# A two-layer graph network with layer norms on one core: closing the rows of four batches by VectorE block turns, transfers over DRAM and GpSimd sums

## The chip, the cores and the metric

The kernel runs on one core of a Trainium2 chip. The metric is the device time of one execution in microseconds (us). A core has TensorE (PE, the matrix engine), VectorE (DVE), ScalarE (ACT), GpSimd (POOL) and SyncE (SP), whose queue issues nearly all DMAs here. Each engine works through its own queue of instructions in order and waits at an instruction until what it needs is there. SBUF is the working memory of 128 partitions, PSUM the accumulators that TensorE writes, in banks of 128 x 512 numbers.

## The reference, cut to what matters

There are 16 batches of 1024 nodes with 128 features, and one 1024 x 1024 adjacency matrix. All is float32.

```python
# layer 0
x = layernorm(x + einsum('nm,bmo->bno', adj, x @ weight) + bias)
# layer 1: five steps of a gated unit; both of its matrices are adj
def step(h):
    m = einsum('nm,bmd->bnd', adj, h)
    av = concatenate([m, m], axis=-1)
    u3 = h @ u3_w.T + u3_b
    z = sigmoid(av @ w3_w.T + w3_b + u3)
    r = sigmoid(av @ w4_w.T + w4_b + u3)
    hv = tanh(av @ w5_w.T + w5_b + (r * h @ u5_w.T + u5_b))
    return (1 - z) * h + z * hv
h = x
for _ in range(5): h = step(h)
out = layernorm(x + h)
```

The last line is what the change concerns: the state `h` after five steps is added to `x`, the result of layer 0, and each node's 128 features are normalized.

## The kernel before, in words

**Tiling.** Four batches make a quad, and there are four quads. Layer 0 runs over the quads first and leaves its result in DRAM (`saved`). Then, for each quad q, layer 1 runs its steps s = 0 to 4. A step is an aggregation over all four batches (`aggregate`, L375) and then, batch by batch (k = 0 to 3), the gates and the update of the state (`gates` L472, `update` L483).

**Aggregation.** The product with the adjacency matrix uses a fast scheme with seven products in place of eight, on two levels: `aggregate` runs four calls of `chain` (L323), named 12, 3, 67 and 54 after the outer products that they make. A chain has seven inner products in the order 1, 5, 6, 2, 7, 3, 4 (chain 54: 1, 5, 6, 2, 7, 4, 3), each some matmuls at L361. After each product comes its evacuation `after[a]` out of PSUM: copies by ScalarE for products 1, 5, 6, 2 and 4, additions by VectorE for 7 (L351) and 3 (L352). `pb` is one bank that products 6, 7 and 4 share. The operands are sums that VectorE makes (`sums_of`, `outer_sums`, L286 to L321). The last sums, at L411 and L413, write the aggregate `agg`. Its right half of columns (`agg[:, k, HALF:]`) is written only at the end of an aggregation.

**Hooks.** What else is to be issued during an aggregation is passed in as `hooks`: for a chain, and for one of its seven products, a list of calls that are traced just before it ("end": after the last). This sets the program order. A scheduler then orders each engine's queue at compile time: of what it takes to be ready, the earliest in program order goes first, so that later work can move ahead into a gap. `tc.keep_in_program_order` ties an instruction behind the one traced before it on its engine, `pin` does so where `strict[0]` is set, and `tc.issue_after(i)` puts instructions on i's engine behind i.

**Two layouts.** The state lives as `hid`, features on partitions. The aggregation needs `rows`, nodes on partitions. Between steps `turn_rows` (L516) turns 32 x 32 blocks of `hid` with one VectorE instruction (L519) into a buffer (`ypad`), writes it to `turned` in DRAM (L523), and `fetch_rows` (L528) reads it back with four DMAs (L532) in such an order that the 128 x 128 turn is complete. `turn_hidden` (L536, turns at L542) and `fetch_hidden` (L551) go the other way for the state that a new quad starts from.

**Gates and update.** For half h of batch k: a matmul with `u3` into a PSUM bank (L451), copied by ScalarE to `seeded`; a matmul with `w4` on top (L462), a sigmoid (L465), a VectorE product (L466); one with `w3` (L467) and a sigmoid. The update has two matmuls (L479, L480), a tanh (L490) and three VectorE instructions (L496 to L498). The banks that `bank` (L92) hands out are three, for gates, updates and turns together.

**Closing rows.** After the last step of a quad, `finish_early` (L656) loads the batch's rows of layer 0 from `saved` into a buffer `y`. `finish` (L576) turns the state with TensorE, four 128 x 128 transposes by `ident` a half (L566), into a bank, and VectorE adds that to `y` (L574). `normalize` (L580) calls `layernorm` (L233): on VectorE eight pairs of `bn_stats` (L240) and `bn_aggr` (L242), on GpSimd four small instructions that make `rstd` and `shift` (L245 to L248), and the application in eight pieces. It goes onto the list `waiting` for ScalarE (L251), of which `drain` (L279) issues three, or one, after each product; with "DVE" it goes to VectorE at once (L261). The store (L257) follows. Batch 0 is closed in s=4 of its own quad, between update 1 and gates 3 (L748). Batches 1 to 3 are closed in s=0 of the next quad through hooks (L718 to L725). The last quad has an ending of its own (`ending`, L660), which keeps its turns and has the only large GpSimd instructions (L679, L680).

## Time and profile before

| what | value |
|---|---|
| three runs | 1811.39, 1811.89, 1814.22 us; median 1811.89 |
| the profiled execution | 1811.78 us, of which the span from first to last instruction is 1810.0 |
| TensorE's granted clock | 0.998 of full speed |
| TensorE turns for closing (L566) | 120 matmuls of 128 x 128, a duration of 281 ns each |
| VectorE additions of them (L574) | 30 of 128 x 512, 675 to 681 ns on average |
| VectorE turns to rows (L519) | 48 of 128 x 1024, 1248 ns; 32 of 128 x 512, 713 ns |
| VectorE turns to hidden of a new quad (L542, into `first`) | 48 of 128 x 256, 415 ns |
| GpSimd `rstd` (L246) | 31 of 128 x 8, 1758 ns |
| write to `turned`, median to landing | 512 KB, 3.8 us |
| fetch from `turned`, median to landing | 128 KB, 2.8 us |
| load of `ypad` from `saved`, median to landing | 512 KB, 3.8 us |

A line of the profile names the source line, the engine, the operation, the tile written and those read (out<-in), the shape, and the count. In a timeline the first number is the start in us from the span's start, the second the time until the group's last instruction ends. In brackets stands how long the engine was idle before it, and what ended that. Matmuls overlap with one another, so the time that one holds TensorE is the distance to the next one's start, not its duration.

### The profile page before, as it was taken

Reading aid. Unit: us, or ns where it says so; the run is one execution under the profiler, and the core shown is the slowest. Engines: PE = TensorE matmul, PEld = TensorE weight load, DVE = VectorE, ACT = ScalarE, POOL = GpSimd, SP = SyncE. Lnnn points to the kernel's source line nnn. Section 1 sums busy time; section 2 is a strip of 40 time slices with the busy share of each in tenths; the row PEclk is TensorE's granted clock in tenths of the full one; section 3 lists DMA queues with packets and bytes.
Section 4 is the critical chain, followed back from the end, with each engine's and each line's share of the span. In section 5 each row is a group of like instructions: output and inputs, shape, how many; then the busy total and the mean of one; then the engine's idle time right before and its main releaser. Section 6 shows DMA issues by size and latency. Waiting matters only on the chain.

```text
span 1810.0 us, 19922 instructions
## 1 busy us (share of the span) xinstructions
PE 1787.7 (99%) x6805; PEld 1269.2 (70%) x6805; DVE 1293.8 (71%) x2316; ACT 793.4 (44%) x1418; POOL 98.0 (5%) x142
## 2 busy tenths in 40 slices
PE   8999999999999999999999999999999999999998
PEld 7888884866758576675857757586675858667584
DVE  7987776676766958576676957667577775767667
ACT  2345555344342554434244463434434553443426
POOL 0112220000000010000000200000000100000004
PEclk9999999999999999999999999999999999999999
DMA  6233262140323334132142423214043331403222
GB/s 224 71 128 138 95 158 68 32 93 12 82 47 93 91 97 93 23 71 51 43 106 81 93 70 70 62 32 93 12 105 95 92 83 23 93 18 76 52 54 82
DMA packets 352564, 140.37 MB, mean 78 GB/s; under 512 B 338128, under 2 KB 339024, under 8 KB 352464
## 3 DMA queue, kind: packets, MB, share of 16 engines
q1 hardware_dynamic: 351600, 135.96, 29.5%
q10 hardware_dynamic: 864, 3.15, 0.4%
q8 instruction: 54, 0.88, 0.2%
q14 instruction: 46, 0.38, 0.1%
HBM read 80.35 MB, written 58.72 MB: 77 GB/s over the span
## 4 chain that ended last, share of the span: by engine, by line
PE 87%; DVE 7%; DMA 2%; ACT 1%; POOL 1%; issue 1%; SPq 0%; DVEq 0%; POOLq 0%
PE pb L361 23%; PE pa L361 13%; PE pc L361 12%; PE pu L462 7%; PE pu L451 7%; PE seeded L467 7%; PE ph L480 7%; PE ph L479 7%; PE pc_x L361 2%; PE pa_x L361 2%; PE seeded L428 1%; DMA rows<-saved 1%; POOL rstd L246 1%; PE pt L566 1%; DVE agg L411 1%
## 5 line engine op out<-in xcount | busy, mean ns | idle before, releaser
L361 PE MATMUL pb<-e,inner 128*128 128x256 f32 x864 | 206.7, 380 | 3.7 <-ACT pb L347 2.6
L466 DVE TENSOR_TENSOR tsum<-tsum,hid 128x512 f32<-128x512 f32 x160 | 107.1, 683 | 114.6 <-ACT tsum L465 114.2
L361 PEld LDWEIGHTS pb<-e,inner 128*128 128x128 f32 x864 | 167.1, 194 | 24.6 <-ACT pb L347 4.2
L490 ACT ACTIVATE tsum<-ph,bh 128x512 f32<-128x512 f32 x158 | 108.6, 687 | 145.0 <-PE ph L480 144.8
L462 PE MATMUL pu<-agg,w_t 128*128 128x512 f32 x320 | 166.0, 608 | 0.5 <-DVE agg L411 0.5
L480 PE MATMUL ph<-tsum,u_t 128*128 128x512 f32 x320 | 163.5, 592 | 0.1
L496 DVE TENSOR_TENSOR tsum<-tsum,hid 128x512 f32<-128x512 f32 x158 | 108.1, 684 | 77.6 <-ACT tsum L490 77.4
L479 PE MATMUL ph<-agg,w_t 128*128 128x512 f32 x320 | 163.5, 592 | 0.0
L467 PE MATMUL seeded<-agg,w_t 128*128 128x512 f32 x320 | 161.0, 592 | 0.0
L451 PE MATMUL pu<-hid,u_t 128*128 128x512 f32 x320 | 152.0, 594 | 2.0 <-DVE ypad L574 2.0
L361 PE MATMUL pb<-s,inner 128*128 128x256 f32 x576 | 151.3, 385 | 0.3 <-DVE agg L351 0.2
L361 PE MATMUL pb<-a,inner 128*128 128x256 f32 x576 | 144.6, 379 | 0.0
L465 ACT ACTIVATE tsum<-pu,br 128x512 f32<-128x512 f32 x160 | 110.2, 688 | 74.3 <-PE pu L462 69.9
L361 PE MATMUL pc<-e,inner 128*128 128x256 f32 x560 | 134.3, 379 | 0.3 <-DVE inner L288 0.3
L361 PEld LDWEIGHTS pb<-s,inner 128*128 128x128 f32 x576 | 108.7, 194 | 24.8 <-DVE rows L351 10.7
L470 ACT ACTIVATE tsum<-seeded,bz 128x512 f32<-128x512 f32 x160 | 109.9, 687 | 27.2 <-PE seeded L467 23.6
L361 PEld LDWEIGHTS pb<-a,inner 128*128 128x128 f32 x576 | 111.5, 194 | 14.1 <-issue 1.9
L361 PEld LDWEIGHTS pc<-e,inner 128*128 128x128 f32 x560 | 108.8, 195 | 12.3 <-PE pa L361 0.6
L498 DVE TENSOR_TENSOR hid<-hid,tsum 128x512 f32<-128x512 f32 x158 | 109.0, 690 | 10.1 <-DVE tsum L497 0.5
L480 PEld LDWEIGHTS ph<-tsum,u_t 128*128 128x128 f32 x320 | 60.7, 190 | 77.0 <-issue 72.9
L467 PEld LDWEIGHTS seeded<-agg,w_t 128*128 128x128 f32 x320 | 60.8, 190 | 76.6 <-issue 76.6
L479 PEld LDWEIGHTS ph<-agg,w_t 128*128 128x128 f32 x320 | 60.5, 190 | 75.4 <-issue 72.7
(181 smaller groups left out, 2859.3 us busy)
## 6 DMA issues: line engine op xcount, KB each, us to landing
turned<-ypad SPq DMA_DIRECT2D x48, 512.0 KB, 3.8
rows<-turned SPq DMA_DIRECT2D x192, 128.0 KB, 2.8
rows<-saved SPq DMA_DIRECT2D x20, 512.0 KB, 3.4
hid<-hidden SPq DMA_DIRECT2D x64, 128.0 KB, 3.4
turned<-ypad SPq DMA_DIRECT2D x32, 256.0 KB, 2.9
rows<-turned SPq DMA_DIRECT2D x128, 64.0 KB, 2.1
hid<-in_x_dram SPq DMA_DIRECT2D x12, 512.0 KB, 4.2
hidden<-first SPq DMA_DIRECT2D x24, 256.0 KB, 3.0
```

What stands on the lines that cost most here:

```text
L361: product = nc.tensor.matmul(bank_of[a][:, ts(o, QT)], chunk(a, o, c), left[n][a][:, c, :], start=(a in (1, 5) and o == 0 and c == 0), sto ...
L451: pin(nc.tensor.matmul(pu, w_t["u3"], hid[:, k, ts(h, HALF)], start=True, stop=True, skip_group_check=True))
L462: pin(nc.tensor.matmul(pu, w_t["w4"], agg[:, k, cols], start=False, stop=True, skip_group_check=True))
L465: pin(nc.scalar.activation(rh[:, cols], pu, AF.Sigmoid, bias=br))
L466: pin(nc.vector.tensor_mul(rh[:, cols], rh[:, cols], hid[:, k, cols]))
L467: pin(nc.tensor.matmul(pz, w_t["w3"], agg[:, k, cols], start=False, stop=True, skip_group_check=True))
L470: pin(nc.scalar.activation(z[:, cols], pz, AF.Sigmoid, bias=bz))
L479: pin(nc.tensor.matmul(ph, w_t["w5"], agg[:, k, cols], start=True, stop=False))
L480: pin(nc.tensor.matmul(ph, w_t["u5"], rh_of[k % 2][:, cols], start=False, stop=True))
L490: pin(nc.scalar.activation(hv, ph, AF.Tanh, bias=bh))
L496: pinned(nc.vector.tensor_sub(hv, hv, hid[:, k, cols]))
L498: pinned(nc.vector.tensor_add(hid[:, k, cols], hid[:, k, cols], hv))
```

## The change

For the first three quads, the closing turns leave TensorE. The state is turned by `turn_rows` as between steps, fetched back from `turned` into a buffer of its own (`close_fetch`, into `ypad`), and GpSimd adds it, in two halves, to the rows loaded from `saved` (`close_load`, `close_add`). `close` then calls `layernorm`. The buffers of the sums are now `hvs`, two pieces of `agg`'s right half, and `ypad[0]`. The places change too: in s=4 batches 0 and 1 are turned, fetched, loaded and summed, and batch 2 is turned. In s=0 of the next quad, hooks of chain 12 turn batch 3, fetch, load and sum batches 2 and 3, and issue the four `fetch_hidden` at products 2, 3 and 4 and the end; batches 1 and 2 are normalized at products 1 and 6 of chain 67, with their statistics pinned; batches 3 (applied on VectorE) and 0 after update 0. That update's `turn_rows` uses `first[:, 0]` in place of `ypad[0]`. VectorE's evacuations in chains are put behind the last statistic closed so far. `turn_hidden` makes one turn of 128 x 1024 and one DMA a batch where it made four turns and two DMAs. The last quad's ending stays as it was.

```diff
@@ def layernorm(y, tag, store, now=False):
-        n = y.shape[1]
+        if len(y.shape) == 4:
+            n = y.shape[1] * y.shape[2]
+            chunk = lambda c: y[:, c // y.shape[2], c % y.shape[2]]
+        else:
+            n = y.shape[1]
+            chunk = lambda c: y[:, c, :]
...
-                pin(nc.vector.bn_aggr(mv[:, c - 1, :], stats[:, c - 1, :]))
+                last_stats[0] = pin(nc.vector.bn_aggr(mv[:, c - 1, :], stats[:, c - 1, :]))
@@ def chain(...):
-            with tc.high_priority():
+
+            behind = tc.issue_after(closed[0].ins) if closed[0] else nullcontext()
+            with tc.high_priority(), behind:
                 after[a]()
@@ def update(tag, k, back=True, spare=False):
         if back and k < 3:
-            turn_rows(k)
+            turn_rows(k, stage=first[:, 0] if spare else None)
@@ def turn_rows(k, h=None, stage=None):
         cols, n = half_of(h)
-        t = ypad[k % 2][:, cols]
+        t = (ypad[k % 2] if stage is None else stage)[:, cols]
@@ def fetch_rows(k, h=None, dst=None):
         cols, n = half_of(h)
+        dst = rows[:, k] if dst is None else dst
         src = between(k, h).rearrange("(to n) (s j) x -> to j (n s) x", n=n, s=4)
         for to in range(4):
             tc.keep_in_program_order(nc.sync.dma_start(
-                rows[ts(to, SQ), k, cols].rearrange("j (m x) -> j m x", x=64), src[to]
+                dst[ts(to, SQ), cols].rearrange("j (m x) -> j m x", x=64), src[to]
             ))
@@ def turn_hidden(k, stage):
-        v = rows[:, k].rearrange("p (n c a j) -> p n c a j", n=4, c=2, a=4)
-        for f in range(2):
-            t = stage(f)
-            for a in range(2):
+        v = rows[:, k].rearrange("p (n c a j) -> p a n c j", n=4, c=2, a=4)
+        if len(stage) == 1:
+            t = stage[0].rearrange("p (a n i c) -> p a n c i", a=4, n=4, c=2)
+            nc.vector.transpose(t, v)
+        for f, t in enumerate(stage):
+            w = 4 // len(stage)
+            for a in range(w) if w < 4 else ():
                 nc.vector.transpose(
                     t[:, ts(a, QT)].rearrange("p (n i c) -> p n c i", n=4, c=2),
-                    v[:, :, :, 2 * f + a],
+                    v[:, w * f + a],
                 )
...
-    y_of = [ypad[0], ypad[1], hvs.rearrange("p h x -> p (h x)"), ypad[0]]
-
-    def finish_early(q, k):
-        nc.sync.dma_start(y_of[k], saved_rows(q * QUAD + k))
-        finish(q, k, y_of[k])
+    def pair(t):
+        return t.rearrange("p (u x) -> p u x", u=2)
+
+    y_of = [hvs, agg[:, 0:2, HALF:], agg[:, 2:4, HALF:], pair(ypad[0])]
+
+    def in_halves(b, src):
+        return src[b].rearrange("(p u c) d -> p u (c d)", u=2, c=CH)
+
+    def close_load(q, k):
+        src = saved[q * QUAD + k].rearrange("p (u x) -> p u x", u=2)
+        tc.keep_in_program_order(nc.sync.dma_start(y_of[k], src))
+
+    def close_fetch(k):
+        fetch_rows(k, dst=ypad[k % 2])
+
+    def close_add(k):
+        t = ypad[k % 2].rearrange("p (u n d c) -> p u n c d", u=2, n=2, c=2)
+        y = y_of[k].rearrange("p u (n c d) -> p u n c d", n=2, c=2)
+        for u in range(2):
+            tc.keep_in_program_order(nc.gpsimd.tensor_add(y[:, u], y[:, u], t[:, u]))
+
+    def close(q, k, now=False):
+        b = q * QUAD + k
+        store = in_halves(b, out).rearrange("p u (c d) -> p u c d", c=CH)
+        strict[0] = k in (1, 2)
+        layernorm(y_of[k].rearrange("p u (c d) -> p u c d", c=CH), f"1_{b}", store, now)
+        strict[0], closed[0] = False, last_stats[0]
@@ the loop over steps, s == 0 and q > 0
                     outer_sums(rows)
-                    before = [call(finish_early, q - 1, k) for k in range(QUAD)]
-                    norm = [call(normalize, q - 1, k, y_of[k]) for k in range(QUAD)]
-                    fetch = [call(fetch_hidden, k) for k in range(QUAD)]
+                    p = q - 1
                     hooks = {
-                        12: {5: [before[1]], 2: [fetch[0], before[2]], "end": [fetch[1], before[3]]},
-                        3: {1: [fetch[2]], 2: [fetch[3]]},
-                        67: {6: [norm[1]], 7: [norm[2]], 4: [norm[3]]},
-                        54: {"end": [call(drain, 99, 0)]},
+                        12: {
+                            1: [call(turn_rows, 3), call(close_fetch, 2)],
+                            5: [call(close_load, p, 2), call(close_add, 2)],
+                            6: [call(close_fetch, 3)],
+                            2: [call(fetch_hidden, 0)],
+                            7: [call(close_load, p, 3), call(close_add, 3)],
+                            3: [call(fetch_hidden, 1)],
+                            4: [call(fetch_hidden, 2)],
+                            "end": [call(fetch_hidden, 3)],
+                        },
+                        3: {},
+                        67: {1: [call(close, p, 1)], 6: [call(close, p, 2)]},
+                        54: {},
                     }
...
+            if last:
+                close_load(q, 0)
             gates(tag, 1)
-            update(tag, 0, not last)
-            if not last:
+            update(tag, 0, not last, s == 0 and q > 0)
+            if s == 0 and q > 0:
+                close(q - 1, 3, "DVE")
+                close(q - 1, 0)
+            if last:
+                turn_rows(0)
+                close_fetch(0)
+                close_add(0)
+            else:
                 fetch_rows(0)
             gates(tag, 2)
             update(tag, 1, not last)
             if last:
-                finish_early(q, 0)
-                normalize(q, 0, y_of[0])
+                turn_rows(1)
                 for k in range(2):
-                    turn_hidden(k, lambda f: first[:, k, ts(f, HALF)])
+                    turn_hidden(k, [first[:, k]])
             else:
                 fetch_rows(1)
             gates(tag, 3)
             if last:
                 sums_of(rows, (1, 2))
                 sums_of(rows, (3,))
                 for k in range(2):
-                    turn_hidden(2 + k, lambda f: first[:, k, ts(f, HALF)])
+                    turn_hidden(2 + k, [first[:, k]])
+                close_fetch(1)
+                close_load(q, 1)
+                close_add(1)
             update(tag, 2, not last)
+            if last:
+                turn_rows(2)
             update(tag, 3, not last)
```

## The prediction, made before the result was known

> **What bounds the kernel now.** I read the busy shares and the chain first, then stages by the table of windows, then the timeline where the changed work lies.
>
> ```profile
> PE 1787.7 (99%) x6805; PEld 1269.2 (70%) x6805; DVE 1293.8 (71%) x2316; ACT 793.4 (44%) x1418; POOL 98.0 (5%) x142
> PE 87%; DVE 7%; DMA 2%; ACT 1%; POOL 1%; issue 1%; SPq 0%; DVEq 0%; POOLq 0%
> ```
>
> TensorE (PE) is the bound, and its work is 87% of the chain. So a PE instruction that goes away counts in full, if nothing that replaces it makes PE wait. What closing rows costs is read from stages: a plain step, then the last step of the first quad (s=4), then the first step of the next (s=0).
>
> ```profile
> 467.17:544.34 77.17, 77.17 (x277) 53.32 (x276) 52.84 (x75) 31.45 (x52) 0.00 (x0) 1.00 0.25 55
> 544.34:620.77 76.43, 75.84 (x279) 53.20 (x278) 58.58 (x112) 29.41 (x49) 3.23 (x4) 1.00 0.40 101
> 620.77:703.62 82.85, 82.85 (x307) 55.81 (x306) 58.47 (x122) 45.66 (x87) 7.38 (x12) 1.00 0.34 85
> ```
>
> Columns: length, then busy time of PE, weight loads, VectorE (DVE), ACT, POOL, the clock, the DMA share, GB/s. The two closing steps take 76.43+82.85 = 159.28 us; two plain ones take 154.34. The excess is 4.94 us. At the other two changes of quads it is 76.15+82.85-154.34 = 4.66 and 77.57+82.86-154.34 = 6.09. Sum **15.7 us**: all that closing costs today on the bound. The timeline shows what it is made of:
>
> ```profile
> 606.93 1.11 PE L566 MATMUL pt<-ident,hid 128*128 128x128 f32 x8
> 607.88 1.12 PE L451 MATMUL pu<-hid,u_t 128*128 128x512 f32 x2
> 609.51 1.12 PE L451 MATMUL pu<-hid,u_t 128*128 128x512 f32 x2 [0.51 <-DVE ypad L574]
> ...
> 622.50 1.11 PE L566 MATMUL pt<-ident,hid 128*128 128x128 f32 x8
> 623.45 1.24 PE L361 MATMUL pc<-e,inner 128*128 128x256 f32 x5
> ```
>
> Eight turns hold PE from 606.93 to 607.88, and from 622.50 to 623.45: 0.95 us a batch, four a quad, 12 in all: 11.4 us. The rest, 4.3 us, is waiting: two L451 take 1.63 us (607.88 to 609.51) where two of that shape take 0.86 elsewhere, as PE waits for a PSUM bank that the turn holds until VectorE has added it (L574).
>
> **What the Trainium skill says.** "TensorE: Matmul & The Clock Gate", Part 4: a TensorE turn does a full 128x128, into PSUM, and needs a VectorE copy after it; the trace agrees (L566, then L574). "VectorE: DVE Perf Modes", The three transpose paths: VectorE turns 32x32 blocks only; hence the trip over DRAM. The trace has such turns (L519, 1248 ns for 128x1024). "SBUF — State Buffer", Who interferes with whom: a VectorE instruction with two SBUF inputs and a GpSimd (POOL) one that reads SBUF shut each other out. The trace agrees where both meet, in the ending:
>
> ```profile
> 1792.33 1.59 POOL L679 TENSOR_TENSOR first<-tsum,hid 128x512 f32<-128x512 f32 x1 [0.77 <-ACT tsum L470]
> 1793.14 1.33 DVE L466 TENSOR_TENSOR tsum<-tsum,hid 128x512 f32<-128x512 f32 x1 [0.35 <-ACT tsum L465]
> 1795.57 1.26 POOL L679 TENSOR_TENSOR first<-tsum,hid 128x512 f32<-128x512 f32 x1
> ```
>
> L466 takes 0.69 alone and 1.33 beside POOL; the POOL product takes 1.26 beside instructions with one input and 1.59 beside L466.
>
> **The change part by part.**
>
> *Turns of 12 batches removed from PE:* 12 x 0.95 = -11.4 us, and with the bank waits -15.7 us. All of it is on the path. Nothing new is put on PE, so the floor is 1811.8 (the profiled execution, 1810.0 of it span; the median is 1811.89) - 15.7 = 1796.1.
>
> *VectorE, per quad.* Removed: 8 additions from PSUM (two take 1.28: 5.1 us), 16 turns of 128x256 in `turn_hidden` (four take 1.43: 5.7). Added: 4 `turn_rows` (1.25 each: 5.0), 4 turns of 128x1024 for hidden (5.0, priced by the same row, the axis order being different), 8 `tensor_scalar` for batch 3 (four took 1.11 at L261: 2.2). Together 12.2 - 10.8 = +1.4 us, of no weight where it is spread. It moves, however: statistics of batch 0 (8 pairs, 2.3 us) leave s=4, which is the tightest place (VectorE 94% busy in its gates, 29.97 of 31.77 us in the table of windows), and those of 3 and 0 may fall in the gates of s=0. There VectorE is busy 25.17 of 34.92 us. There is cover before that too: with the sums and statistics of batches 1 to 3 done at 646.77, VectorE idles for long:
>
> ```profile
> 650.83 0.69 DVE L351 TENSOR_TENSOR rows<-pb,rows 128x512 f32<-128x512 f32 x1 [3.76 <-PE pb L361]
> ...
> 662.92 0.69 DVE L351 TENSOR_TENSOR rows<-pb,rows 128x512 f32<-128x512 f32 x1 [4.47 <-PE pb L361]
> ...
> 666.43 0.69 DVE L466 TENSOR_TENSOR tsum<-tsum,hid 128x512 f32<-128x512 f32 x1 [2.82 <-ACT tsum L465]
> ```
>
> Only batches 1 and 2 are pinned in program order, so those of 3 and 0 can float into these gaps. I take 0.3 us a quad, 0.9 in all; from 0 to 9.9 (rival B). `tensor_scalar` also waits for POOL's `rstd` (0.24+1.67 us); in a gap that costs nothing.
>
> *POOL sums:* 24 of 128x512, 1.26 to 1.6 us each, 30 to 38 us on an engine 5% busy. What counts is the lock: each can delay one VectorE addition by up to 1.33-0.69 = 0.64 us, 15.4 us in all if every delay reached PE, nothing if none does (a gain is excluded, since nothing else leaves POOL). A delay reaches PE only where VectorE is what PE waits for: in the plain weight-load waits that is mainly L351 (23 times) and L411 (17 times in 20 steps), so about one in ten: 1.8 us.
>
> *ACT:* batch 3 is applied on VectorE, 24 applications of 0.42 us less; ACT, 44% busy, is not the bound: 0.
>
> *DMA.* Per quad 4 writes and 16 fetches between SBUF and `turned` are added; the loads from `saved` and the stores stay. A plain step makes 4 such trips at a share of 0.25: 19.3 us of all engines. The two closing steps use 0.40x76.43+0.34x82.85 = 58.7 of 159 us; after it about 78 (49%). No queue fills up; what counts is lateness. On SyncE's (SP's) queue 20 issues of 0.38 to 0.48 us, some 9 us, stand among those of `fetch_hidden`, whose result is first used at 662.65, 42 us after the step's start: hidden.
>
> *The new waits.* Let T be the start of s=0 (620.77). `hid` of batch 3 is final at T+6.3 (627.0), its turn at T+7.5. SP waits for that turn first, since its write is issued ahead of the fetch of batch 2: fetch issued T+7.9 to T+9.9, landed T+12.7 (2.8), load from `saved` landed T+14.2 (3.8), two POOL sums T+17.4. SP then waits for POOL before loading batch 3 into the buffer batch 2 was fetched to: T+21.2, sums T+24.4. VectorE's queue is in order: statistics of 1 and 2 stand ahead of evacuation 7 of chain 67. That chain now starts at T+18.3 (21.1 less three turns), product 7 ends 5 x 1.72 later, at T+26.9; with 2.3 us of statistics, batch 2's sum may come as late as T+24.6. It comes at T+17.4: 7 us of slack. Behind the waiting instruction stand VectorE's evacuations, and PE behind those. Cost 0. The store of batch 2 leaves in chain 54, about T+36, and the buffer in `agg` is written at T+44: hidden.
>
> *Sum:* 1811.8 - 15.7 + 0.9 + 1.8 = 1798.8; **1799**.
>
> **Rivals.**
> A (0.60): as computed, 1796 to 1803.
> B (0.17): VectorE becomes the bound at the end of s=0. Statistics of 3 and 0 (4.6) and the `tensor_scalar` (2.2) all run after update 0, where the idle gaps left are 1.58+1.86 = 3.4 us: 3.4 us a quad reach the next step's sums. In place of the 0.3 taken above: 1798.8 + 3 x 3.1 = 1808. For it: program order puts them there. Against: they are ready earlier, and today's statistics already run some 10 us ahead of their place.
> C (0.08): every POOL lock reaches PE: 1796.1 + 15.4 = 1811.5, no difference. Against: VectorE has 29% idle time.
> D (0.15), slower: batch 2's (or a floated batch 3's) sum comes late, and VectorE's queue stands still with evacuation 7 behind it. It decides from T+24.6 on, each us counting three times; slower by over 0.2% needs 6.4 us more, T+31. If the 16 hidden fetches (16 x 0.48 = 7.7 us of issue, and 9.6 of transfer, half of a trip's 4.8 for each batch) stand ahead in SP's queue, the sum comes at T+34.7, 10.1 us late: 1798.8 + 30.3 = 1829. For it: SP's queue is in order, and the scheduler's estimate of landings decides what stands ahead. Against: six of the 16 are issued by T+4 today, and none of the new fetches waits for them by its data.
>
> **How the numbers follow.** 0.2% (3.6 us) is about what a measurement of this kernel can tell from no change. Faster: A and B, 0.77; same: C, 0.08; slower: D, 0.15. The range runs from the floor, 1796, over A, B and C to 1813; D and a little of the tails stay out. A alone is 1796 to 1803.
>
> **What would show it.** Right: L566 counts 24; the two closing steps take 155 to 156 us together; PE waits of L451 on `ypad` gone; POOL sums of 1.3 to 1.6 us. B: the first sums of s=1 late, PE waiting for `inner`. D: a VectorE idle stretch ahead of `bn_stats`, released by POOL. Wrong altogether: a wait for `hid` at the gates of s=0.

## The result, and the profile after

| what | before | after |
|---|---|---|
| median, range | 1813.06 us, 1811.39 to 1814.33 (4 runs) | 1859.75 us, 1857.85 to 1863.28 (4 runs) |
| the profiled execution, its span | 1811.78, 1810.0 | 1863.28, 1861.5 |
| TensorE turns for closing | 120 (L566) | 24 (now L579) |
| TensorE's granted clock | 0.998 | 0.984 |

The ratio is 1.026, interval 1.0242 to 1.0279: slower by 2.6%, where 1799 us, 0.7% less than the 1811.89 of before, was forecast. Source lines from 235 on have moved: the matmul of a chain is L368 now (it was L361), the evacuations by VectorE L358 and L359, the first gate matmul with the aggregate L471, the last sums into `agg`'s right half L420, `rstd` L251 and `shift` L252 and L253, the turn in `turn_rows` L528, its write L532, the fetch L542, the load from `saved` L679, GpSimd's sum L688.

The busy shares and the chain of the kernel after:

```profile
PE 1797.7 (97%) x6709; PEld 1268.4 (68%) x6709; DVE 1307.0 (70%) x2292; ACT 783.8 (42%) x1394; POOL 143.4 (8%) x166
PE 82%; DVE 10%; DMA 3%; POOL 2%; issue 1%; ACT 1%; SPq 0%; DVEq 0%; POOLq 0%
```

TensorE has 96 instructions fewer and is yet busy 10 us longer; on the chain it went from 87% to 82%, and VectorE, DMA and POOL took its place. So TensorE waits for them, and part of its own work has become slower. The table of windows by stage (a plain step, s=4, s=0, s=1 of the first change of quads; columns as before) says where:

```profile
467.80:544.96 77.16, 77.16 (x277) 53.32 (x276) 52.77 (x77) 31.46 (x53) 0.00 (x0) 1.00 0.25 55
544.96:619.59 74.63, 74.60 (x271) 52.18 (x270) 56.07 (x82) 29.52 (x50) 2.90 (x2) 1.00 0.43 107
619.59:721.33 101.74, 87.24 (x281) 56.89 (x280) 64.58 (x144) 38.60 (x70) 22.59 (x23) 0.92 0.46 103
721.33:799.35 78.02, 78.02 (x279) 53.70 (x278) 53.62 (x78) 35.06 (x62) 0.00 (x0) 1.00 0.26 61
```

s=4 fell from 76.43 to 74.63: the turn is gone and its bank wait with it. (s=1 is longer by 0.86 only because two gate matmuls moved over the border between the stages.) s=0 rose from 82.85 to 101.74, and to 100.82 and 100.64 at the other changes. TensorE stands idle in it for 14.50 us, in three places, each of them in every change of quads. First TensorE's waits over the whole run (who waits, for whom: us in total, times, longest), then the three in TensorE's timeline:

```profile
PE pb L368 <- DVE rows L358: 15.6, 3, 5.5
PE pb L368 <- DVE first L358: 12.3, 3, 4.6
PE pu L471 <- POOL shift L252: 9.8, 2, 4.9
PE pu L471 <- POOL shift L253: 5.3, 1, 5.3
```

```profile
635.37 3.78 PE L368 MATMUL pb<-a,inner 128*128 128x256 f32 x8 [4.64 <-DVE first L358]
662.98 2.07 PE L368 MATMUL pb<-s,inner 128*128 128x256 f32 x4 [4.59 <-DVE rows L358]
692.71 2.05 PE L471 MATMUL pu<-agg,w_t 128*128 128x512 f32 x2 [5.27 <-POOL shift L253]
```

I call them **wait 1** (chain 12, evacuation 7), **wait 2** (chain 67, evacuation 7) and **wait 3** (the gates). Count: 82.85 less three turns of 0.95 and the 0.86 moved to s=1 is 79.1; 14.5 of idle makes 93.6. Of the remaining 8.1, the greater part is slow matmuls, in the second column of these lines and in the lines that follow each of them. Eight matmuls of this form take 1.89 elsewhere and 3.78 here, four take 1.03 elsewhere and 2.07 here. After each of these three waits TensorE runs at about half speed for a while.

VectorE's timeline shows what it did while TensorE waited:

```profile
618.56 1.66 DVE L506 TENSOR_TENSOR tsum<-tsum 128x512 f32<-128x512 f32 x1
...
631.22 1.24 DVE L528 STREAM_TRANSPOSE ypad<-hid 128x1024 f32<-128x1024 f32 x1
632.38 0.65 DVE L295 TENSOR_TENSOR inner<-tsum 128x512 f32<-128x512 f32 x1
633.13 1.58 DVE L296 TENSOR_TENSOR inner<-tsum,inner 128x512 f32<-128x512 f32 x1
634.64 0.68 DVE L358 TENSOR_TENSOR first<-pb,first 128x512 f32<-128x512 f32 x1
...
646.33 0.69 DVE L298 TENSOR_TENSOR inner<-tsum,inner 128x512 f32<-128x512 f32 x1 [0.30 <-PE pb L368]
...
647.54 1.25 DVE L528 STREAM_TRANSPOSE ypad<-hid 128x1024 f32<-128x1024 f32 x1
...
659.81 0.49 DVE L245 BATCH_NORM_STATS2 stats<-agg 128x6 f32<-128x128 f32 x2 [9.34 <-POOL agg L688]
...
662.25 0.67 DVE L358 TENSOR_TENSOR rows<-pb,rows 128x512 f32<-128x512 f32 x1
```

Wait 1: VectorE works without a pause up to 634.64, the turn of batch 2 and two instructions stretched beside GpSimd among it. Wait 2: VectorE itself stands for 9.34 us at batch 2's statistics, and evacuation 7 (662.25) is behind them; the change ties it there (`issue_after(closed[0].ins)` in `chain`). GpSimd's and SP's timelines tell why that sum is late:

```profile
627.38 6.79 POOL L688 TENSOR_TENSOR agg<-agg,ypad 128x512 f32<-128x512 f32 x2 [7.71 <-DVE tsum L506]
...
658.50 2.52 POOL L688 TENSOR_TENSOR agg<-agg,ypad 128x512 f32<-128x512 f32 x2 [5.32 <-DMA agg<-saved]
```

```profile
632.48 0.38 SPq L532 DMA_DIRECT2D turned<-ypad  x1
632.92 1.29 SPq L567 DMA_DIRECT2D hid<-hidden  x1
648.82 0.38 SPq L532 DMA_DIRECT2D turned<-ypad  x1
649.28 3.65 SPq L542 DMA_DIRECT2D ypad<-turned  x4
653.03 0.54 SPq L679 DMA_DIRECT2D agg<-saved  x1
```

Between 634.21 and 648.82 SP issues nothing: it stands at the write of turn 3, which VectorE makes only at 647.54. The fetch of batch 2 stands behind it, though the write of its data was issued at 632.48, and such a write lands after 3.8 us in the median.

Wait 3, in VectorE's timeline again: the last sums into `agg` come after the statistics of batches 3 and 0 and the applications of batch 3, with a wait for `rstd` between.

```profile
684.54 1.12 DVE L266 TENSOR_SCALAR ypad<-ypad,mv,rstd 128x128 f32<-128x128 f32 x4 [1.68 <-POOL rstd L251]
...
688.51 0.29 DVE L247 BATCH_NORM_AGGREGATE mv<-stats 128x2 f32<-128x6 f32 x2
...
691.91 2.50 DVE L420 TENSOR_TENSOR agg<-rows 128x512 f32<-128x512 f32 x4
```

The list of waits names POOL's `shift` for wait 3; the gate's operand comes from L420, which begins without any idle time before it: it had only its place in the queue to wait for. "PSUM — Partial Sum Buffer" of the Trainium skill, Engine vs sequencer instructions, says that the queues of ScalarE, VectorE and GpSimd are strict FIFO (first in, first out); the trace agrees with it for VectorE, which stood for 9.34 us: TensorE had ended product 7 of chain 67 at 654.93, and its evacuation went at 662.25, after the statistics.

### The profile page after: what moved, and what is told of

It reads as the page before. It is cut to its first block, busy times and chain, and to the rows that moved or that the text cites. A ratio compares the mean times of both kernels' runs of the same rounds, so it can differ in the third digit from the quotient of the medians.

```text
span 1861.5 us, 19832 instructions
## 1 busy us (share of the span) xinstructions
PE 1797.7 (97%) x6709; PEld 1268.4 (68%) x6709; DVE 1307.0 (70%) x2292; ACT 783.8 (42%) x1394; POOL 143.4 (8%) x166
## 4 chain that ended last, share of the span: by engine, by line
PE 82%; DVE 10%; DMA 3%; POOL 2%; issue 1%; ACT 1%; SPq 0%; DVEq 0%; POOLq 0%
PE pb L368 22%; PE pa L368 12%; PE pc L368 12%; PE pu L471 7%; PE seeded L476 6%; PE ph L489 6%; PE ph L488 6%; PE pu L460 6%; PE pc_x L368 2%; PE pa_x L368 2%; POOL rstd L251 1%; PE seeded L437 1%; DMA agg<-saved 1%; DVE stats L245 1%; DVE tsum L506 1%
## 5 line engine op out<-in xcount | busy, mean ns | idle before, releaser
L368 PE MATMUL pb<-e,inner 128*128 128x256 f32 x864 | 207.7, 381 | 3.1 <-ACT pb L354 2.6
L471 PE MATMUL pu<-agg,w_t 128*128 128x512 f32 x320 | 169.2, 618 | 15.6 <-POOL shift L252 9.8
L368 PEld LDWEIGHTS pb<-e,inner 128*128 128x128 f32 x864 | 167.6, 195 | 24.2 <-ACT pb L354 4.4
L475 DVE TENSOR_TENSOR tsum<-tsum,hid 128x512 f32<-128x512 f32 x160 | 107.5, 685 | 101.8 <-ACT tsum L474 101.5
L368 PE MATMUL pb<-s,inner 128*128 128x256 f32 x576 | 154.2, 391 | 15.7 <-DVE rows L358 15.6
L368 PE MATMUL pb<-a,inner 128*128 128x256 f32 x576 | 152.7, 395 | 12.3 <-DVE first L358 12.3
L460 PE MATMUL pu<-hid,u_t 128*128 128x512 f32 x320 | 150.9, 592 | 0.0
L368 PEld LDWEIGHTS pb<-s,inner 128*128 128x128 f32 x576 | 110.1, 197 | 39.9 <-DVE rows L358 26.0
L368 PE MATMUL pc<-e,inner 128*128 128x256 f32 x560 | 136.2, 383 | 0.3 <-DVE inner L295 0.3
L368 PEld LDWEIGHTS pb<-a,inner 128*128 128x128 f32 x576 | 116.3, 203 | 28.1 <-DVE first L358 13.5
L479 ACT ACTIVATE tsum<-seeded,bz 128x512 f32<-128x512 f32 x160 | 109.9, 687 | 28.1 <-PE seeded L476 24.6
L368 PEld LDWEIGHTS pc<-e,inner 128*128 128x128 f32 x560 | 111.3, 199 | 14.7 <-PE pa L368 1.4
L471 PEld LDWEIGHTS pu<-agg,w_t 128*128 128x128 f32 x320 | 55.3, 191 | 90.6 <-ACT seeded L463 41.0
L506 DVE TENSOR_TENSOR tsum<-tsum 128x512 f32<-128x512 f32 x158 | 112.1, 709 | 4.8
```

The lines of the kernel that those rows point to most:

```text
L368: product = nc.tensor.matmul(bank_of[a][:, ts(o, QT)], chunk(a, o, c), left[n][a][:, c, :], start=(a in (1, 5) and o == 0 and c == 0), sto ...
L460: pin(nc.tensor.matmul(pu, w_t["u3"], hid[:, k, ts(h, HALF)], start=True, stop=True, skip_group_check=True))
L471: pin(nc.tensor.matmul(pu, w_t["w4"], agg[:, k, cols], start=False, stop=True, skip_group_check=True))
L479: pin(nc.scalar.activation(z[:, cols], pz, AF.Sigmoid, bias=bz))
L506: pinned(nc.vector.tensor_mul(hv, hv, z[:, cols]))
```

## The experiments

The theory after the result: **each wait comes from an order of instructions**. Work that is late stands in an in-order queue (VectorE's or SP's) ahead of work that TensorE needs; the method of closing costs nothing by itself. The rivals: the additional VectorE work and the lock with GpSimd cost this wherever they are put, or one of the removed forms was the cheaper one.

**e8.** The kernel before, with the one turn of 128 x 1024 in `turn_hidden` alone.

```diff
-        for f in range(2):
-            t = stage(f)
-            for a in range(2):
-                nc.vector.transpose(
+        if len(stage) == 1:
+            t = stage[0].rearrange("p (a n i c) -> p a n c i", a=4, n=4, c=2)
+            nc.vector.transpose(t, v)
```

> The kernel before with one part of the change alone: one turn of 128x1024 and one DMA a batch in turn_hidden in place of four turns and two DMAs. Every theory: 0.2 us of VectorE less a batch and nothing on PE's path, 1811 to 1814. A gain of over 3 us would say that the gates of s=4 are bound by VectorE.

Measured: 1814.1 us, ratio 1.0001 (0.9992 to 1.0011). By itself this part costs nothing.

**e1.** The fetch of batch 2 ahead of turn 3 in SP's queue.

```diff
-                            1: [call(turn_rows, 3), call(close_fetch, 2)],
+                            1: [call(close_fetch, 2)],
                             5: [call(close_load, p, 2), call(close_add, 2)],
-                            6: [call(close_fetch, 3)],
+                            6: [call(turn_rows, 3), call(close_fetch, 3)],
```

> Only the order of the hooks in chain 12 changes: the fetch and the load of batch 2 are issued on SP's queue ahead of the write of batch 3's turn. Theory (SP's queue stands behind a late turn of batch 3, so batch 2's sum comes late and VectorE's queue stands still in chain 67): the 9.3 us that VectorE waits for GpSimd ahead of batch 2's statistics is gone, PE's wait of 4.6 us at product 4 of chain 67 with it, and the time falls by some 6 us a quad, to about 1841. Rival (batch 2's sum is late because of its own DMAs or of a slow GpSimd): the wait stays and the time is within 3 us of 1860.

Measured: 1844.15 us, ratio 1.0173 (1.0157 to 1.0188). Wait 2 is no longer in the list of waits. e1's timeline of SP:

```profile
636.82 1.90 SPq L542 DMA_DIRECT2D ypad<-turned  x4
...
648.58 0.39 SPq L532 DMA_DIRECT2D turned<-ypad  x1
```

SP issued the fetch of batch 2 at 636.82 instead of 649.28, while the turn of batch 3 still came at 647.30. VectorE's wait ahead of batch 2's statistics shrank from 9.34 to 4.00 us, and what is left no longer reaches TensorE. So it was SP's order that made batch 2 late for TensorE.

**e2.** The last sums into `agg`'s right half ahead of everything of batches 3 and 0.

```diff
-            nc.vector.tensor_add(agg[:, dst, HALF:], a[:, cols], b[:, cols])
+            ready[0] = nc.vector.tensor_add(agg[:, dst, HALF:], a[:, cols], b[:, cols])
@@ the loop over steps
+            late = ExitStack()
+            if s == 0 and q > 0:
+                late.enter_context(tc.issue_after(ready[0].ins))
             gate_half(tag, 0, 1)
...
                 close(q - 1, 0)
+            late.close()
```

> Only VectorE's order in the first step of a quad changes: the gates, update 0 and the closing of batches 3 and 0 are put behind the last sums into agg. Theory (the sums into agg's right half stand, by the compiler's order, behind statistics and the wait for rstd, because agg's right half was lent as a buffer): PE's wait of 5.3 us at L471 goes, 6 to 7 us a quad with the slower clock after it, and the time falls to about 1841. Rival (the stores out of agg really land so late): VectorE waits there for a DMA instead, and the time stays at 1860 or rises.

Measured: 1847.57 us, ratio 1.019 (1.0173 to 1.0207). This is 12.2 us less than after, where 19 were expected. Wait 3 is gone, but the work that was moved away appears later. Two lines of e2's list of waits, with counts that after doesn't have:

```profile
PE pb L368 <- DVE inner L296: 5.0, 5, 1.5
PE pc L368 <- DVE inner L295: 2.9, 4, 1.0
```

`inner` are the first sums of step s=1: that is rival B of the prediction, 7.9 us in three changes (s=1 takes 80.0 in the first).

**e3.** e1 and e2 together.

> The two edits together. If the two waits are separate, their gains add: about 1822, with the wait at product 4 of chain 12 (4.6 us a quad, and a slower clock after it) left over, still 9 us slower than before. If one wait only uncovers the other, it ends near the better of the two single edits.

Measured: 1828.03 us, ratio 1.0086 (1.0071 to 1.0101). The gains add, and a little more: 15.6 and 12.2 us alone, 31.7 together. Left are wait 1 (11.9 us in three) and e2's 8.

**e4.** After, with GpSimd's sums cut to 8 of 512 columns. This kernel leaves out most of the addition of the state, and keeps every transfer, turn and wait.

```diff
-            tc.keep_in_program_order(nc.gpsimd.tensor_add(y[:, u], y[:, u], t[:, u]))
+            tc.keep_in_program_order(nc.gpsimd.tensor_add(y[:, u, 0, :, :4], y[:, u, 0, :, :4], t[:, u, 0, :, :4]))
```

> GpSimd's sums take 8 of the 512 columns of each half and leave the others out, so that the rows that are normalized lack most of the state; all transfers, turns, waits and statistics stay. Theory (the lock between GpSimd's sums and VectorE's additions is a side cost): VectorE's additions in the last gates of s=4 and in chain 12 return to 0.69 us, the wait at product 4 of chain 12 shrinks from 4.6 to 2 or 3 us, the other two stay, and the time is 1848 to 1856. Rival (the lock is what makes sums and steps late): all three waits shrink and the time is under 1830.

Measured: 1841.54 us, ratio 1.0161 (1.0142 to 1.0179), 18.2 us less than after: below the theory's range, and above the rival's. All three waits shrink (12.3 to 5.2, 15.6 to 7.8 and 15.1 to 13.2 us in three changes) and none goes. e4's timeline of TensorE:

```profile
632.27 1.99 PE L368 MATMUL pb<-a,inner 128*128 128x256 f32 x8 [2.04 <-DVE first L358]
655.36 2.08 PE L368 MATMUL pb<-s,inner 128*128 128x256 f32 x4 [2.96 <-DVE rows L358]
...
684.88 1.77 PE L471 MATMUL pu<-agg,w_t 128*128 128x512 f32 x2 [4.39 <-POOL shift L252]
```

Part of the gain is speed: after the wait of 2.04 the eight matmuls take 1.99, not 3.78. The turn of batch 3 came at 640.95, earlier than in after (647.54) and still far from the forecast place. In both traces it stands close behind the same operand sum of chain 3 (L298, at 640.35 here and 646.33 in after), and its buffer had been free for some 13 us (since 628.17 here, 634.17 in after, the ends of batch 1's sums). So it was the place in VectorE's queue that set its date, and not the buffer.

**e12.** The orders of e3 and the sums of e4.

> The two orders of e3 (fetch and load of batch 2 ahead of turn 3 in SP's queue; the last sums into agg's right half ahead of the statistics of batches 3 and 0) and the sums of e4 together: GpSimd adds only 8 of the 512 columns of each half, so most of closing's additions are left out. It asks whether order and sums account for the whole loss. Own theory: what is left in e3 is the wait in chain 12 (11.9 us in three) and the waits for operand sums in s=1 (8 us); small sums take chain 12's wait away for the most part (e4: from 4.64 to 2.04 each, and without the slow products that follow a long wait) and shorten the rest: 1808 to 1818. Rival (e4's gain came through the waits that e3 has removed, so the two overlap): 1822 to 1828.

Measured: 1816.28 us, ratio 1.0011 (1.0004 to 1.0019), 11.7 less than e3, and inside the expected range. Orders and sums account for nearly the whole loss against the kernel before, but not for the gain that was forecast: that is still missing.

**e10.** After, with `nc.vector` in place of `nc.gpsimd` in `close_add`. (Waits (b) and (c) in the text below are waits 2 and 3.)

> The kernel after with one edit: VectorE makes the sums of closing (a row of layer 0 plus the turned state) in place of GpSimd; places in program order, DMAs and waits as they are. It adds 8 sums of 0.7 us each to VectorE per quad, 16.6 us in all, and takes away every lock between GpSimd's sums and VectorE. Own theory: turn 3 still comes late and agg's right half is still lent, so waits (b) and (c), some 14 us and 15 us, stay, and what the lock costs (e4: 18 us for sums and their length together) comes back in good part as VectorE's own work: 1845 to 1862. Rival (the lock by itself is the cause of the slowdown): under 1838. A third: VectorE's queue now stands itself at a sum whose DMA has not landed, as it did at statistics: over 1870.

Measured: 1863.67 us, ratio 1.028 (1.0258 to 1.0301), just above the expected range. The three waits are all there with no large GpSimd sum left:

```profile
PE pu L471 <- DVE agg L420: 16.7, 4, 5.4
PE pb L368 <- DVE rows L358: 14.4, 3, 5.8
PE pb L368 <- DVE first L358: 9.4, 3, 3.6
```

So the waits don't need the lock, and GpSimd was no worse a place for the sums than VectorE. What the lock costs can't be read from this run, since it also adds 16.6 us of work to VectorE. Wait 3 is now put down to L420 itself.

**e5, e6, e7.** Three repairs on top of e3 that missed. In e5 the turn of batch 2 and the load and sum of batch 1 go behind evacuation 7 of chain 12. In e6 batch 0 is closed in chain 67 of s=1 instead. e7 is both.

```diff
+    def turn_late():
+        with tc.issue_after(evac[7].ins):
+            turn_rows(2)
...
+                            3: [turn_late, call(close_load, p, 1), call(close_add, 1)],
...
+                if s == 1 and q > 0:
+                    hooks[67] = {1: [call(close, q - 1, 0)]}
```

> On top of both orders: VectorE's turn of batch 2 is put behind the evacuation of product 7 of chain 12, and GpSimd's sum of batch 1 (with its load) behind that turn; the fetch of batch 2 and the turn of batch 3 follow, and batch 2's statistics move from product 6 to product 3 of chain 67. Theory (the wait of PE in chain 12 is VectorE's backlog, made by the early turn and by the lock with the sum of batch 1): PE's wait of 4.1 us and the slower clock after it go, 6 us a quad, from 1828 to about 1810. Rival (the backlog comes from the gates of s=4, which the change left as full as before): PE's wait stays at 2 us or more, and the time stays above 1820.

> On top of both orders: batch 0 is closed in chain 67 of the next step instead of after update 0. Theory (with the other waits gone, the statistics and the application of batches 3 and 0 make VectorE late for the first sums of s=1): PE's waits for inner at the start of s=1 (5.0 and 3.0 us in all) shrink to under 1 us a quad, and the time falls by 5 to 8 us from 1828, to 1820 to 1823. Rival (they are late for the store of batch 3 and for SP's queue): no change.

> All four edits. If the turns on TensorE were worth what the stages showed (15.7 us) and every wait is gone, 1797 to 1803, below the kernel before. If something of the new path can't be hidden, between 1803 and 1815, and the profile names it.

Measured: e5 1854.61 us, ratio 1.0231 (1.021 to 1.0252); e6 1830.88, 1.0102 (1.0084 to 1.012); e7 1853.14, 1.0223 (1.0206 to 1.024). Wait 1 halved in e5 (11.9 to 6.0 us), but other waits came: TensorE for ScalarE's evacuations (16.1 and 4.3 us, with 4.3 of the first in e3 already) and 7.5 us at the first gate. A line of e7's timeline of VectorE has the reason (e5 has the same, 13.98):

```profile
657.91 0.69 DVE L475 TENSOR_TENSOR tsum<-tsum,hid 128x512 f32<-128x512 f32 x1 [14.09 <-ACT tsum L474]
```

L475 belongs to the first gate, far ahead; the order at compile time had put it before the statistics of batch 1, and VectorE stood there for 14 us. e6 did not shorten s=0 or s=1 (87.20 and 80.29, in e3 86.89 and 80.01), since batch 0's statistics floated back into the gates of s=0. A place in program order is no place in a queue: each move needs a tie.

**e9.** The same moves, tied. In chain 12 the second half of the outer sums goes behind evacuation 7 too; turn 3 and all that follows it is traced in chain 67; the first gate's VectorE product goes behind the last statistics; batches 3 and 0 are closed in chain 67 of s=1, behind its evacuation 7, both applied by ScalarE. Update 2 of s=0 turns into `first[:, 0]` as well.

```diff
+    def turn_late():
+        with tc.issue_after(evac[7].ins):
+            turn_rows(2)
+            outer_sums(rows, False, True)
+    def close_late(q, k):
+        with tc.issue_after(evac[7].ins):
+            close(q, k)
...
-                            1: [call(turn_rows, 3), call(close_fetch, 2)],
+                            1: [call(turn_rows, 3), call(close_fetch, 3), call(close_load, p, 3),
+                                call(close_add, 3), call(fetch_hidden, 3), call(close, p, 1)],
```

> Every order repaired at once, nothing left out. In chain 12: the second half of its own operand sums and the turn of batch 2 go behind evacuation 7; the load and sum of batch 1 follow the turn. Fetch, load and sum of batch 2 follow at product 4, with fetch 2 ahead of turn 3 in SP's queue; turn 3, its fetch, load and sum are traced in chain 67. The early VectorE product of gate (0,0) is tied behind the last closed statistics, so that it can't stand in front of them; the last sums into agg's right half come before any statistics of batches 3 and 0; these two are closed in chain 67 of step s=1, applied by ACT. Own theory (what costs is where work stands in VectorE's and SP's in-order queues and which buffers are lent, not the turns over DRAM as such): all three waits of after go, s=0 falls from 101 to 80 to 84 us, s=1 to 77 to 79; time 1798 to 1810, so faster than the kernel before. Rival (the additional work on VectorE and the lock with GpSimd bound a quad's change wherever they are put; e3 shows what is left): s=0 stays at 86 or more, time 1825 to 1832. A third outcome, a new stall behind an order that I did not see: over 1835.

Measured: 1820.07 us, ratio 1.0035 (1.0024 to 1.0047). Waits 1 to 3 and those of `inner` are down to some tenths, but s=0 takes 85.62, 84.85 and 84.44: between the theory and its rival. What is left is new, in e9's timeline of TensorE:

```profile
663.84 1.99 PE L368 MATMUL pb<-e,inner 128*128 128x256 f32 x8 [1.28 <-ACT pb L354]
...
678.79 1.94 PE L471 MATMUL pu<-agg,w_t 128*128 128x512 f32 x2 [2.52 <-issue]
```

Gate matmuls (L460) that used to fill the time at the end of the aggregation had floated ahead of products 4 and 6 of chains 67 and 54 (they run from 654.48 and 657.12).

**e13.** e9, with the gates tied behind TensorE's last product, and in s=1 two applications in place of three issued to ScalarE after a product.

```diff
+                    last_product[0] = product
...
-                late.enter_context(tc.issue_after(ready[0].ins))
+                late.enter_context(tc.issue_after(ready[0].ins)); late.enter_context(tc.issue_after(last_product[0].ins))
```

> The kernel of the late closing (e9) with two further orders. In s=0 the gates of batches 0 and 1 are tied behind TensorE's last product traced so far, so that their first matmuls (L460) stand at the end of the aggregation and fill the time while VectorE writes agg's right half, in place of floating ahead of products 4 and 6 of chains 67 and 54; and in s=1 two applications in place of three are issued to ScalarE after a product. Nothing is left out. Own theory: what e9 still loses in a quad's change is TensorE standing for 2.5 us at the first gate and 1.3 us at product 6 of chain 54 in s=0, and 0.8 us in s=1, each from these orders, about 4.6 us times three, 13.8 in all; s=0 falls from 85 to 81 or 82, s=1 to 78: 1805 to 1811, faster than the kernel before. Rival (the closing of four batches fits no order at this cost: each wait repaired returns elsewhere): 1815 or more.

Measured: 1813.19 us, ratio 1.0004 (0.9996 to 1.0013): level with the kernel before, between the expected range and the rival's. Three waits are left in each s=0:

```profile
656.20 1.99 PE L368 MATMUL pb<-e,inner 128*128 128x256 f32 x8 [1.28 <-ACT pb L354]
...
663.16 1.12 PE L471 MATMUL pu<-agg,w_t 128*128 128x512 f32 x2 [0.66 <-ACT seeded L463]
...
668.31 1.56 PE L368 MATMUL pc<-e,tsum 128*128 128x256 f32 x6 [1.44 <-ACT rows L355]
```

Product 5 was missing between 1 and 6; it ran at 664.99. My reading was that its accumulator `pc` is freed by evacuation 3 of chain 67, which stood behind batch 2's statistics (653.66).

**e14.** e13, with these statistics behind that evacuation, and batch 2 applied on VectorE, by a call kept in `deferred` until product 1 of chain 54; the gates wait for product 4 too. VectorE's sum after chain 67 is tied behind the statistics, and its later evacuations behind the applications.

```diff
-                            3: [call(close, p, 2)],
+                            4: [call(close, p, 2, "later")],
...
-                        54: {},
+                        54: {1: [lambda: deferred.pop()()]},
...
-                late.enter_context(tc.issue_after(ready[0].ins)); late.enter_context(tc.issue_after(last_product[0].ins))
+                late.enter_context(tc.issue_after(ready[0].ins)); late.enter_context(tc.issue_after(last_product[0].ins)); late.enter_context(tc.issue_after(by_name[4].ins))
```

> The kernel of e13 with the order of chain 54 in s=0 repaired; nothing is left out. Batch 2's statistics go behind evacuation 3 of chain 67 (L359), so that the accumulator pc is free and product 5 of chain 54 stands between products 1 and 6 again; batch 2 is applied on VectorE, ahead of evacuation 7 of chain 54, in place of eight ScalarE applications that stood between ScalarE's evacuations; and the gates behind the aggregation are tied behind product 4 too. Own theory: the waits that e13 still shows in every change of quads (TensorE for ScalarE at product 6 for 1.28 us, at the first gate for 0.66, at product 3 for 1.44, with some tenths of slow start, some 3.4 to 4 us times three) come from these orders and go: s=0 80.5 to 82, time 1801 to 1806, faster than the kernel before. Rival (VectorE, with two applications more work, now stands for rstd ahead of evacuation 7, and TensorE behind it; each repair returns elsewhere): 1811 or more.

Measured: 1799.9 us (1798.3 to 1800.98), ratio 0.9921 (0.9907 to 0.9935): faster than both kernels, and a little better than expected. Product 5 now runs between 1 and 6 (654.59). e14's windows of the same four stages, and two of its sums on GpSimd:

```profile
469.76:546.92 77.16, 77.16 (x277) 53.31 (x276) 52.77 (x76) 31.45 (x53) 0.00 (x0) 1.00 0.25 55
546.92:621.51 74.59, 74.59 (x271) 52.17 (x270) 56.20 (x81) 29.04 (x50) 2.99 (x2) 1.00 0.43 108
621.51:701.40 79.89, 79.46 (x281) 52.52 (x280) 62.44 (x113) 36.01 (x62) 14.82 (x14) 1.00 0.55 123
701.40:779.42 78.02, 78.02 (x279) 53.70 (x278) 57.79 (x109) 38.18 (x70) 4.71 (x8) 1.00 0.28 68
```

```profile
640.13 3.05 POOL L688 TENSOR_TENSOR agg<-agg,ypad 128x512 f32<-128x512 f32 x2 [19.00 <-DMA agg<-saved]
...
649.71 2.54 POOL L688 TENSOR_TENSOR agg<-agg,ypad 128x512 f32<-128x512 f32 x2
```

s=0 takes 79.89 with the same 281 TensorE instructions as in after, of which 0.43 is idle, and the clock is 1.00. VectorE, GpSimd and the DMAs do all the work of the change. So the method can be placed nearly without a cost on the path; the rival, a cost wherever the work is put, is out. Nor can these orders alone be the gain: s=0 of before has no idle TensorE time that they could save (82.85 of 82.85 busy). Over the whole run TensorE is busy 1776.7 us in e14 and 1787.7 before, 11.0 less, where 12 turns of 0.95 are 11.4.

## Why the prediction was wrong

**What held.** The removal was priced nearly rightly. s=4 lost turn and bank wait. Over s=4, s=0 and s=1 the three changes of quads take 13.2 us less in e14 than before (3.95, 3.97 and 5.32, from the windows), of the 15.7 that the removal was to bring; what the other 0.8 a quad are was not traced. The DMA time came out: 78 us in the two closing steps were forecast, 0.43 x 74.63 + 0.46 x 101.74 = 78.9 were measured. ScalarE got lighter as said (1418 to 1394 instructions).

**The first step that failed** is "Behind the waiting instruction stand VectorE's evacuations, and PE behind those. Cost 0." Its dates were wrong, not its chain of reasons. With T = 619.59: `hid` of batch 3 was final at T+9.4 (T+6.3 in the prediction), but the turn ran at T+28 (T+7.5), the fetch was issued at T+29.7 (T+7.9), and the sum ended at T+41.4 (T+17.4), past the limit of T+24.6 that the prediction had set itself. (Wait 1 had moved that limit too: product 7 of chain 67 ended at T+35.3 and not at T+26.9, so that 4.59 us of wait were left of it.) The prediction let an instruction run as soon as its data is there. The turn needed its buffer as well, which held batch 1's rows until GpSimd had summed them (634.17, T+14.6), and its place in VectorE's queue as compiled came still later, behind chain 3's operand sums. So rival D was the right kind: the trace shows the sign named for it, VectorE idle ahead of the statistics, released by POOL, with evacuation 7 behind. But D blamed the 16 fetches of hidden; what stood ahead in SP's queue was the write of a late turn (e1). And D was one wait of three, so 1829 was too low.

**The second** is "The store of batch 2 leaves in chain 54, about T+36, and the buffer in `agg` is written at T+44: hidden." It was written at T+72, after statistics that had been let ahead of it (e2). Rival B had seen these statistics in the gates and had priced their lateness for the next step, 3.4 us a quad, and that appeared in e2 and e3 (8 us in three); it had not seen that they could stand ahead of the aggregate. That the order came from the lent buffer (the sums into it must wait for stores, so other work seemed ready earlier) is argued only: no run gave batches 1 and 2 another buffer.

**The third** is the lock, 1.8 us. It was counted per VectorE instruction, 0.64 each and one in ten on the path. Measured: up to 0.97 (L506, 1.66 instead of 0.69), and the two sums of batch 1 took 6.79 instead of 2.5. In after the sums are on the path, since VectorE's queue stands at the end of batch 2's and works slowly beside batch 1's: cutting them gave 18.2 us (e4), and 11.7 with two orders repaired (e12); lock and length of the sums were not separated. In e14 the full sums cost nothing that the waits show, though VectorE's sums beside them are stretched there too. So what the lock costs depended on where the sums stood.

**Not in the sum at all:** wait 1. Turns of three batches, the closing sums and the outer sums meet on VectorE around the border of s=4 and s=0, the place that the prediction had called the tightest, and "+1.4 us, of no weight where it is spread" was not followed into chain 12. And the slow TensorE after each wait: 87.24 - 79.46 = 7.8 us in this s=0, against e14, a third of the 21.85 between the two.

Two of the prediction's sums don't fit themselves, and neither decides anything: one lock in ten of 15.4 us is 1.5 and not 1.8, and rival D's "6.4 us more" counts from 1796.1 where its 1829 counts from 1798.8, from which it would be 5.5.

As a price of a free path, 1799 was about right. That e14, which is another kernel, lies so near it, at 1799.9, is in part luck: against before in its own rounds (1814.27) it gained 14.4 us, where 13.0 were forecast. Wrong was the belief that this change's orders leave the path free.

## What to carry to other kernels

Before a step is called hidden, write down for each instruction of it the buffer that it needs, who frees that, and what stands ahead of it in its queue as compiled, not as traced; readiness of data is only the first of three. Take a waiting engine's in-order queue as part of the path of everything behind it, and don't let a pinned DMA stand behind one whose data comes late. When a change moves work off the bound engine and the time rises, repair orders one by one: waits that go uncover the next, and only the last repair here showed the gain.

## What was not expected of the hardware

TensorE ran at half speed after many of its waits, and short ones could suffice. The windows of after around wait 1 and just behind it (632 to 636, then 636 to 640; the number ahead of the DMA share is the granted clock):

```profile
632.00:636.00 4.00, 0.63 (x2) 0.54 (x3) 3.90 (x6) 0.00 (x0) 2.16 (x2) 0.80 0.60 133
636.00:640.00 4.00, 4.00 (x11) 3.19 (x10) 1.33 (x3) 0.59 (x1) 0.00 (x0) 0.50 0.14 31
```

Eight matmuls took 1.99 after a wait of 2.04 (e4), 3.78 after 4.64. In between it is not one threshold, as a line of e12, one of e5 and one of e10 show:

```profile
1026.65 3.68 PE L368 MATMUL pb<-a,inner 128*128 128x256 f32 x8 [2.16 <-DVE first L358]
637.21 1.99 PE L368 MATMUL pb<-a,inner 128*128 128x256 f32 x8 [2.18 <-DVE first L358]
1451.47 1.99 PE L368 MATMUL pb<-a,inner 128*128 128x256 f32 x8 [2.83 <-DVE first L358]
```

In all these traces, from 600 to 1620 us, no wait of up to 2.05 us was followed by slow matmuls, waits from 2.16 to 2.83 sometimes were, and each from 2.96 on was. "TensorE: Matmul & The Clock Gate", Part 1, describes half the clock after an idle window of about 3.4 us that runs freely. Half speed and the loose threshold agree, but here a wait of 2.16 us was enough once (clock 0.53 in the 3.65 us behind it), and the measurement decides. So the three waits of s=0, 14.5 us together, cost about 14.5 + 8.1 = 22.6.

GpSimd's sums of 128x512 took 1.27 each beside VectorE instructions that read at most one operand from SBUF (2.54 for two, at 649.71 in e14), and 3.4 each where VectorE worked without a pause, mainly on sums of two SBUF operands (6.79 for two, at 627.38 in after).
